# A two-layer graph network on one core: B, C and step sizes of the mixer's scan taken into wider products, a bias added by DMA, weights fetched through a ring

## The chip, the core and the metric

The kernel runs on one core of a Trainium2 chip, as one launch. The metric is the device time in microseconds of one execution, and a kernel's time is the median of several runs. The engines are TensorE (PE; its loads of the stationary operand are listed as PEld), VectorE (DVE), ScalarE (ACT), GpSimd (POOL) and SyncE (SP). Each works through a queue of its own in order, and DMAs are issued from the queues of SP and POOL. L637 is line 637 of the kernel before.

## The reference, cut to what matters

There are 32 graphs of 512 nodes with 256 features, and a 512 x 512 adjacency matrix for each. Two layers run one after the other; in each a graph part and a feed-forward part are added to x.

```python
# layer 0
x = x + graph_conv(layernorm(x), adj)                    # relu(x W_upd + mean of neighbours' x W_msg + bias)
t = max_over_features(xn[:, None, :] + Wt) + bt          # "tropical" product, 1024 outputs; xn = layernorm(x)
trop = s * max_k(t*sl_cvx + of_cvx) + (1-s) * min_k(t*sl_ccv + of_ccv)
g = sigmoid(xn @ Wg + bg)
x = x + (g*trop + (1-g)*gelu(xn @ Wc + bc)) @ Wd + bd
# layer 1
x = x + relu(softmax(leaky(masked e_src+e_dst)) @ h + bias) + h   # 4 heads, then a layer norm of each head
fx, xm = xn @ W_fx.T + b_fx, xn @ W_x.T + b_x            # 8 heads of 64
sw = softmax((xm @ W_slice.T + b_slice) / temp)          # each node's share of 64 slices
st = (fx, sw) summed over nodes / (sum of sw + 1e-5)     # 64 slice tokens of 512 features a graph
z, xBC, dt = split(st @ hy_in_w.T)                       # 512, 512+64+64, 2*8 columns, in this order
dt = softplus([dt[:8], flip(dt[8:])] + dt_bias)          # one step size a head and direction
x_, Bm, Cm = split(silu(causal_conv3(xBC)))
y = state-space scan of (dt, Bm, Cm, x_) over the 64 tokens, forward and backward, shifted by one
y = (y + x_ * (x_ @ fcD_w.T + D)) * silu(z)
y = y * rsqrt(mean(y*y) + 1e-5) * norm_w @ hy_out_w.T
x = x + (y handed back to the nodes by sw) @ out_w.T + out_b
```

## The kernel before

**Two layers, woven.** Everything is float32 except masks and adjacency. The program is written with Python generators: `woven` (L66) takes steps from two of them in a given proportion, and so sets the program order. A tile scheduler then places semaphores and may put an instruction of an engine ahead of others that are not ready. `tile_kernel` (L2165) runs `layer0_sorted` (L98), which weaves in the first part of `layer1_plain` (L865) as `following`, and then the rest of `layer1_plain`. Plainer versions of both layers (L705, L1614) stand under a condition at the end and are not entered with this input.

**Layer 0.** The graphs are taken in 4 segments of 8. `convs` makes the graph convolution of a segment, and its nodes are then sorted by how many terms their tropical maximum may need, and written to DRAM (`rows_of`). `feed_forwards` (L543) works on 32 groups of 4 tiles of 128 sorted nodes; a group is `xs`, 128 partitions by 4 rows. Its steps are `sums`, `mixed` and `down`, and the `sums` of the next group are woven with the `mixed` of the present one.

- `sums` (L546) gathers the group's nodes by POOL (L553), normalises them on ACT (xn, L574), and gathers for each node the row of a table that belongs to its largest feature (`best`, L564). For as many further terms as a tile needs (its cap less one) a row is gathered (`rows`, L595, four buffers) and taken into the maximum by DVE (L598). Last, POOL adds the bias bd of the final product to the four tiles one by one (L609 and L610). The normalised copy has been read by then, so that x + bd stands ready for the final sum.
- `mixed` (L613) computes for each 128 of the 1024 hidden features the two products (L623), their activations (L625), the transposed maximum (tz), the bends of the convex and concave functions (L632, L636 on ACT and L637 on DVE) and the gate's mixture.
- `down` (L645) multiplies by Wd (po, L652), DVE adds po to `xs`, and SP writes the group to `x2s`.

**Set-up of layer 1.** In `following` the constants of layer 1 come by SP's queue, each with a wait for its buffer. `load_T` (L999) takes a weight matrix in pieces of 128 rows: a DMA of up to 256 KB on SP's queue to one of two buffers (`raw512` and others), up to four PE transposes, and a copy by ACT. It is called for W_fx (4 pieces), hy_in_w (10, the last with 16 rows), hy_out_w (4), out_w (2) and fcD_w (1), with a yield after each piece. Then the small ones follow: W_slice, W_x and their biases, from which `wsl` is made (L1051). `add_rows` (L947) adds a constant row to a graph's x with one accumulating DMA from DRAM on POOL's queue (L949), whose source is a [2, 4 x 256] tile read by all partitions.

**Layer 1.** `attentions` goes through the graphs; `mixer` (L1580) through 16 groups g of two graphs. For each `want` that the mixer yields, credit times PACE steps of `attentions` are taken (end of `layer1_plain`), so that attention of later graphs fills the places where a mixer's step waits for another engine. The parts:

- `prepare` (L1155) gathers x, makes the attention's operands and, by PE, the mask (`maskp`, L1091).
- `attention` (L1223) goes in turns over pairs of heads q and blocks j of 128 neighbours. `weigh` (L1215) makes two weights `att` (L1220, DVE). After the last pair of a block, 12 matrix products are issued: eight into `avp` (L1256) and four into `adp` (L1261), in the order in which the weights were made. `norm` (L1289) follows some steps later.
- `slices` (L1325) makes the softmax over slices and `tokens` (L1365) the slice tokens uT.
- `scan` (L1390) is the mixer's recurrence, written as matrix products for both graphs of a group at once. Its order on PE is: xp, the x columns (L1407); bcp, B and C as two 64-column products (L1416); dtp, the step sizes (L1435, 32 records of 8 columns that put each head's direction in its place, and L1400); zp, the gate's 512 columns (L1400); then, after other work, gp = B C (L1494); segp, the summed logarithms (L1498); xtp and qp, which need the convolved x; yp (L1524); yTp; oTp (L1542); msp, the mean square spread over partitions (L1550); and vp. On DVE and ACT: softplus of the step sizes (Exp at L1450, Ln at L1456, and four DVE operations between); Silu of z (L1462); the four x convolutions of three taps (xT, each with a Silu); the convolutions of B and of C (bcT, cpad) on 64 partitions, each with a Silu; la and seg (L1488); decay (Exp of segp); mix and its three products; y and its products; the copies of yT and oT; and rms by POOL's power (after L1553).
- `unslice` (L1569) hands the result to the nodes (outp, L1574), and SP writes the graph out.

The few lines on which the prediction's steps rest are the bias loop, the step sizes and the attention's order:

```python
                for t in range(NT):
                    nc.gpsimd.tensor_add(xg[:, t, :D], xg[:, t, :D], bd)
...
            tok_matmul(pd[:, 2 * H : 4 * H], DT0, 2 * H)
            nc.vector.tensor_add(v, pd[:, : 4 * H], dtb.rearrange("p i h -> p (i h)"))
...
                    for p in range(AP):
                        for k in range(2 * HO // HW):
```

Of the kernel before, what the change touches and what calls it, by code (L numbers as in the profile page):

```python
# [8 lines left out]
F32 = mybir.dt.float32  # L9
# [4 lines left out]
AF = mybir.ActivationFunctionType  # L14
# [5 lines left out]
P = 128  # L20
# [77 lines left out]
def layer0_sorted(tc, ident, eps, x, adj, w, x2s, ranks, over, following):  # L98
# [29 lines left out]
    with ExitStack() as ctx:  # L128
# [12 lines left out]
        bd = const("bd", [P, D], w["bd"].partition_broadcast(P))  # L141
# [35 lines left out]

        table = dr.tile([D, FFN], F32, tag="table", name="table", bufs=1)
# [364 lines left out]
        def feed_forwards():  # L543


            def sums(s, g):  # L546
# [62 lines left out]
                for t in range(NT):  # L609
                    nc.gpsimd.tensor_add(xg[:, t, :D], xg[:, t, :D], bd)  # L610
# [254 lines left out]
def layer1_plain(tc, ident, eps, x2s, ranks, adj, w, out, over, ps):  # L865
# [35 lines left out]
    with ExitStack() as ctx:  # L901
# [58 lines left out]
        bc_w = const("bc_w", [S, 2, KW], w["hy_conv_w"][DI:].rearrange("(c p) k -> p c k", p=S))  # L960
        bc_b = const("bc_b", [S, 2], w["hy_conv_b"][DI:].rearrange("(c p) -> p c", p=S))
        skip = const("skip", [P, H], w["hy_D"].partition_broadcast(P))
        dtb = ctile("dtb", [P, 4, H])
        for i in range(4):
            nc.sync.dma_start(dtb[:, i, :], w["hy_dt_bias"].partition_broadcast(P))
# [31 lines left out]
        with tc.tile_pool(name="raw", bufs=2, side="right") as raw:  # L997

            def load_T(dst, src, name):  # L999

                R, Ccols = src.shape
                for r0 in range(0, R, P):
                    n = min(P, R - r0)
                    t = raw.tile([P, Ccols], F32, tag=f"raw{Ccols}", name=f"{name}_{r0}")
                    nc.sync.dma_start(t[:n], src[r0 : r0 + n, :])
                    pt = psum("tp", f"{name}p{r0}").rearrange("p (c r) -> p c r", r=P)
                    cs = Ccols // P
                    for c in range(cs):
                        nc.tensor.transpose(pt[:, c, :n], t[:n, c * P : (c + 1) * P], ident[:n, :n])
                    nc.scalar.copy(dst[:, :, r0 : r0 + n], pt[:, :cs, :n])  # L1010
                    yield

            yield from load_T(wfxT, w["W_fx"], "wfx")
            yield from load_T(inT, w["hy_in_w"], "in")
            yield from load_T(hoT, w["hy_out_w"], "ho")
            yield from load_T(owT, w["out_w"], "ow")
            yield from load_T(fcT, w["hy_fcD_w"], "fc")
# [5 lines left out]
            def twice_T(src, name):  # L1023

                R, Ccols = src.shape
                t = raw.tile([P, 2, Ccols], F32, tag="twice", name=name)
                for i in range(2):
                    nc.sync.dma_start(t[:R, i, :], src)
                pt = psum("tp", f"{name}p")
                nc.tensor.transpose(pt[:, :R], t[:R].rearrange("p i c -> p (i c)"), ident[:R, :R])  # L1030
                return pt


            wsT = raw.tile([P, G], F32, tag="wsT", name="wsT")
            nc.vector.tensor_copy(wsT, twice_T(w["W_slice"], "ws")[:, :G])
            wx = raw.tile([P, KC, D], F32, tag="wx", name="wx", bufs=1)
            nc.sync.dma_start(wx, w["W_x"].rearrange("(k p) d -> p k d", p=P))
            bx = raw.tile([P, KC], F32, tag="bx", name="bx")
            nc.sync.dma_start(bx, w["b_x"].rearrange("(k p) -> p k", p=P))
            bsl = raw.tile([1, H, G], F32, tag="bsl", name="bsl", bufs=1)  # L1040
            bs = raw.tile([1, G], F32, tag="bs", name="bs")
            nc.sync.dma_start(bs, w["b_slice"].rearrange("(o n) -> o n", o=1))
# [22 lines left out]
            for c in range(DC):  # L1065
                sq = raw.tile([P, H * G], F32, tag="wsl2", name=f"wsl2_{c}")
                nc.vector.tensor_mul(sq, wsl[:, c, :], wsl[:, c, :])
                nc.tensor.matmul(pn, ones, sq, start=c == 0, stop=c == DC - 1)
# [154 lines left out]
        def attention(b):  # L1223
# [21 lines left out]
            for i, (q, j) in enumerate(turns):  # L1245
# [5 lines left out]
                if q + 1 == AP:  # L1251
                    ends = dict(start=j == 0, stop=j == NT - 1)
                    for p in range(AP):
                        for k in range(2 * HO // HW):
# [5 lines left out]
                    for h in range(AH):  # L1260
# [129 lines left out]
        def scan(g, uT):  # L1390
# [14 lines left out]
            for k in range(KC):  # L1405
                for c in range(KC):
                    nc.tensor.matmul(px[:, k * T : (k + 1) * T], inT[:, c, DI + k * P : DI + (k + 1) * P],  # L1407
                                     uT[:, c, :], start=c == 0, stop=c == KC - 1)
# [3 lines left out]
            pb = psum("any", f"bcp{g}")  # L1412
            for i in range(2):
                c0 = 2 * DI + i * S
                for c in range(KC):
                    nc.tensor.matmul(pb[:S, i * T : (i + 1) * T], inT[:, c, c0 : c0 + S], uT[:, c, :],  # L1416
                                     start=c == 0, stop=c == KC - 1)
            bpad = sb.tile([S, 2, GB, LP], F32, tag="bpad", name=f"bpad{g}", bufs=1)
            nc.gpsimd.memset(bpad[:, :, :, : KW - 1], 0.0)
            nc.scalar.copy(bpad[:, :, :, KW - 1 :],  # L1420
                           pb[:S, : 2 * T].rearrange("p (k j l) -> p k j l", k=2, j=GB))
# [9 lines left out]
            pd = psum("any", f"dtp{g}")  # L1431
            for j in range(GB):
                for i in range(2):
                    for c in range(KC):
                        nc.tensor.matmul(pd[i * G : (i + 1) * G, j * H : (j + 1) * H],  # L1435
# [811 lines left out]
```

## Time and profile before

The page describes one profiled execution.

| what | value |
|---|---|
| median of 3 runs, us | 4365.9 (4364.42 to 4366.94) |
| profiled execution, us | 4372.35, its span 4370.6 |
| granted clock of PE, mean of the span | 0.955 |
| instructions in the span | 57973 |
| DMA packets | 244051, 507.52 MB, mean 116 GB/s |
| queue of POOL's software DMAs | 349.50 MB, 26.7% of the 16 engines' time |
| queue of SP's DMAs | 154.21 MB, 11.3% |
| rows gathered, L595 | 212 by 1166 ns of POOL |
| maximum, L598 | 212 by 1290 ns of DVE, idle before it 121.4 us |

The span is the time from the first to the last instruction. A row of instruction groups gives the line, the engine, the operation, the written tile and what it reads, how often it ran, its busy time, the mean duration of one in ns, and the idle time of its engine just before it with what ended most of this. The page's slices cut the span into 40 equal parts, and each digit is the busy share in tenths. In a timeline a row gives the start in us, the busy time, the engine, the line, the tiles, the shape and the number of instructions. A matrix product of the program shows as two records on PE; the tables count records.

### The profile page before, as it was taken

How to read it: one execution, taken by the hardware profiler on the slowest of the kernel's cores; microseconds unless marked ns; L12 is line 12 of the kernel's file. 1: busy time of each engine (PE TensorE's matmuls, PEld its weight loads, DVE VectorE, ACT ScalarE, POOL GpSimd, SP SyncE). 2: the span in 40 equal slices, each digit the busy share in tenths (PEclk: the TensorE clock that was granted, in tenths of full speed). 3: DMA queues.
4: the chain of work that ended last, by engine and by line, in shares of the span. 5: the costliest groups of instructions: out<-in, count | busy, mean ns of one | idle time of the engine just before them, and what ended most of it. 6: DMA issues, size and time to landing. Idle time of an engine off the chain costs nothing.

```text
span 4370.6 us, 57973 instructions
## 1 busy us (share of the span) xinstructions
PE 3882.4 (89%) x20311; PEld 2456.1 (56%) x20311; DVE 3279.3 (75%) x7008; ACT 2295.0 (53%) x4756; POOL 1617.9 (37%) x2036
## 2 busy tenths in 40 slices
PE   5567898988989999888998899999999999999997
PEld 4454565565655666554555455655555555555555
DVE  6668887898878978877775777777777777777763
ACT  3345655566655656546564555555554455554533
POOL 2346644665536644354431322222222222222210
PEclk8778999999999999998999999999999999999998
DMA  5546543564436644375441322222222322222200
GB/s 128 160 154 216 179 156 126 165 218 143 153 117 199 199 156 135 93 250 167 147 133 40 95 73 73 69 65 72 68 68 76 78 75 78 64 74 77 61 25 21
DMA packets 244051, 507.52 MB, mean 116 GB/s; under 512 B 39299, under 2 KB 114827, under 8 KB 243748
## 3 DMA queue, kind: packets, MB, share of 16 engines
q0 software_dynamic: 107904, 349.50, 26.7%
q1 hardware_dynamic: 135844, 154.21, 11.3%
q8 instruction: 162, 2.65, 0.2%
q14 instruction: 141, 1.16, 0.1%
HBM read 446.46 MB, written 57.17 MB: 115 GB/s over the span
## 4 chain that ended last, share of the span: by engine, by line
DVE 33%; PE 32%; DMA 11%; issue 9%; POOL 8%; ACT 5%; SPq 0%; another core or an unknown queue 0%; DVEq 0%; POOLq 0%; ACTq 0%
DVE att L1220 4%; DVE acc L637 4%; PE clsp L623 4%; PE gatep L623 3%; PE po L652 3%; PE avp L1256 3%; DMA rows<-table,xs 2%; DVE best L598 2%; DMA rows<-table,tops 2%; DVE sw L1349 2%; DVE sst L1347 2%; PE yTp L1354 2%; DVE sw L1344 2%; PE oTp L1542 1%; DMA best<-table,xs 1%
## 5 line engine op out<-in xcount | busy, mean ns | idle before, releaser
L623 PE MATMUL clsp<-xnT,wc 128*128 128x512 f32 x1024 | 521.8, 628 | 55.5 <-ACT cls L625 39.7
L623 PE MATMUL gatep<-xnT,wg 128*128 128x512 f32 x1024 | 502.1, 609 | 10.5 <-ACT gate L625 9.7
L652 PE MATMUL po<-wd,acc 128*128 128x256 f32 x2048 | 456.9, 382 | 6.5 <-DVE acc L641 3.5
L652 PEld LDWEIGHTS po<-wd,acc 128*128 128x128 f32 x2048 | 388.8, 191 | 73.1 <-issue 9.2
L1220 DVE SCALAR_TENSOR_TENSOR att<-own,other,mask 128x512 f32<-128x512 f32 x512 | 366.1, 744 | 76.4 <-DMA own<-ownd 76.4
L637 DVE SCALAR_TENSOR_TENSOR acc<-past,fld,acc 128x512 f32<-128x512 f32 x448 | 346.3, 776 | 28.3 <-ACT past L636 20.3
L598 DVE SCALAR_TENSOR_TENSOR best<-rows,xs,best 128x1024 f32<-128x1024 f32 x212 | 273.1, 1290 | 121.4 <-ACT best L592 75.8
L632 ACT ACTIVATE acc<-tz,fld 128x512 f32<-128x512 f32 x256 | 199.0, 778 | 269.1 <-PE tz L630 237.5
L623 PEld LDWEIGHTS gatep<-xnT,wg 128*128 128x128 f32 x1024 | 197.3, 197 | 254.0 <-issue 200.8
L636 ACT ACTIVATE past<-tz,fld 128x512 f32<-128x512 f32 x448 | 291.6, 694 | 73.6 <-DVE acc L637 72.1
L595 POOL DMA_INDIRECT rows<-table,xs x212 | 247.3, 1166 | 176.7 <-DVE best L598 121.8
L1256 PE MATMUL avp<-att,hv 128*32 128x512 f32 x2048 | 297.4, 599 | 6.1 <-DVE att L1220 6.1
L623 PEld LDWEIGHTS clsp<-xnT,wc 128*128 128x128 f32 x1024 | 182.6, 199 | 195.2 <-issue 114.3
L434 PE MATMUL pm<-h,adj 128*128 128x258 f32 (+1 forms) x1024 | 178.9, 321 | 100.3 <-DVE keep L427 34.4
L625 ACT ACTIVATE gate<-gatep,fld 128x512 f32<-128x512 f32 x256 | 175.6, 686 | 153.4 <-PE gatep L623 130.4
L1342 PE MATMUL lgp<-wsl,x4T 128*128 128x512 f32 x512 | 241.4, 610 | 14.3 <-ACT sw L1343 6.7
L1354 PE MATMUL yTp<-sw,x 128*128 128x512 f32 x512 | 237.0, 602 | 17.4 <-DVE sw L1349 16.9
L1161 POOL DMA_INDIRECT x<-x2s,ranks x128 | 135.2, 1056 | 295.5 <-DVE att L1220 147.5
L553 POOL DMA_INDIRECT xs<-rows_of,order x128 | 158.8, 1241 | 229.7 <-DVE acc L637 111.8
L1307 POOL TENSOR_TENSOR mu<-mu,eps 128x16 f32<-128x16 f32 x32 | 111.3, 3478 | 350.4 <-DVE mu L1306 350.4
L1574 PE MATMUL outp<-v,swT 128*128 128x256 f32 x1024 | 227.6, 381 | 0.0
L625 ACT ACTIVATE cls<-clsp,fld 128x512 f32<-128x512 f32 x256 | 176.3, 689 | 94.4 <-PE clsp L623 59.1
(598 smaller groups left out, 8809.0 us busy)
## 6 DMA issues: line engine op xcount, KB each, us to landing
adj<-in_adj POOLq DMA_DIRECT2D x128, 256.0 KB
ai<-in_adj SPq DMA_DIRECT2D x128, 256.0 KB
x<-added POOLq DMA_DIRECT2D x64, 512.0 KB
own<-ownd SPq DMA_DIRECT2D x128, 256.0 KB
rows_of<-keep SPq DMA_DIRECT2D x32, 550.0 KB
x<-in_x SPq DMA_DIRECT2D x32, 512.0 KB
x2s<-xs SPq DMA_DIRECT2D x32, 512.0 KB
out<-x SPq DMA_DIRECT2D x32, 512.0 KB
```

The source lines that it names most:

```text
L595: nc.gpsimd.indirect_dma_start(out=row, out_offset=None, in_=table, in_offset=bass.IndirectOffsetOnAxis(ap=idxs[:, k : k + 1].bitcast(U32) ...
L598: nc.vector.scalar_tensor_tensor(m, row, vals[:, k : k + 1], m, ALU.add, ALU.max)
L623: nc.tensor.matmul(pf, wf[:, c, f * P : (f + 1) * P], xnT[:, c, :], start=c == 0, stop=c == DC - 1)
L625: nc.scalar.activation(o, pf, fn, bias=fld[:, f, bf : bf + 1], scale=1.0 if fn == AF.Gelu else 0.5)
L636: nc.scalar.activation(r, z, AF.Relu, bias=fld[:, f, AT + b : AT + b + 1])
L637: nc.vector.scalar_tensor_tensor(y, r, fld[:, f, CH + b : CH + b + 1], y, ALU.mult, ALU.add)
L652: nc.tensor.matmul(po[:, i, :], acc[f][:, t * P : (t + 1) * P], wd[:, f, :], start=f == 0, stop=f == FC - 1)
L1220: nc.vector.scalar_tensor_tensor(e, own[h], other[:, j, h : h + 1], mask[:, j, :], ALU.max, ALU.mult)
L1256: nc.tensor.matmul(pv[p][k * HW : (k + 1) * HW, :], hv[:, j, h, e : e + HW], weighed[b, h, j], **ends)
L1342: nc.tensor.matmul(pf, xnT[:, c, t * P : (t + 1) * P], wsl[:, c, :], start=c == 0, stop=c == DC - 1)
L1354: nc.tensor.matmul(py, xn[:, t, c * P : (c + 1) * P], sw[:, t, :], start=t == 0, stop=t == NT - 1)
L1574: nc.tensor.matmul(po[:, :D], swT[:, k, t * P : (t + 1) * P], v[:, k, :], start=k == 0, stop=k == KC - 1)
```

## The change

It has four parts.

1. **Layer 0's last bias.** bd is put into a DRAM tile of four rows at the start. Instead of four POOL additions a group, one accumulating DMA a group is issued by POOL: its source is read by all partitions, and it writes four pieces of 256 elements on each partition, since a row of `xs` is longer than its 256 features.
2. **Layer 1's weights.** One list of 21 pieces replaces the calls of `load_T`. Their buffers are a ring of five, and the DMA of a piece is issued three pieces ahead of its use. In `inT` the columns of the step sizes come first, so that they lie next to the gate's. W_x, W_slice and their biases are asked for ahead of the pieces.
3. **Attention.** The 12 products of a block are issued in the reverse order of the weights: the weight made last is read first.
4. **The mixer's scan.** B and C are one product of 128 columns. The 16 step-size columns and the first 256 of the gate are one product of 272 columns into the same PSUM bank as B and C, and the other 256 are a product into a second bank. The 32 records of 8 columns go. DVE adds the bias to the 16 columns once and puts the four 64 x 8 blocks for the directions in place by four small additions. The convolution of B and C is one on 128 partitions instead of two on 64, and stands ahead of x's in the program; Silu of z is taken in two halves, and both stand ahead of all of these. gp's and yp's products alternate between the two graphs. The msp products go; four small DVE operations put the mean square in place instead.

The diff, cut to its core:

```diff
-        bd = const("bd", [P, D], w["bd"].partition_broadcast(P))
+        bd = dr.tile([NT, D], F32, tag="bd", name="bd", bufs=1)
+        nc.sync.dma_start(bd, w["bd"].partition_broadcast(NT))
...
-                for t in range(NT):
-                    nc.gpsimd.tensor_add(xg[:, t, :D], xg[:, t, :D], bd)
+                nc.gpsimd.dma_start(xg[:, :, :D], bd.partition_broadcast(P), accum_op=ALU.add)
...
+            wx = raw.tile([P, KC, D], F32, tag="wx", name="wx", bufs=1)
+            nc.sync.dma_start(wx, w["W_x"].rearrange("(k p) d -> p k d", p=P))
+            twice = raw.tile([P, 2, w["W_slice"].shape[1]], F32, tag="twice", name="ws", bufs=1)
...
-            yield from load_T(wfxT, w["W_fx"], "wfx")
-            yield from load_T(inT, w["hy_in_w"], "in")
-            yield from load_T(hoT, w["hy_out_w"], "ho")
-            yield from load_T(owT, w["out_w"], "ow")
-            yield from load_T(fcT, w["hy_fcD_w"], "fc")
+            pieces = [(dst, src, r0)
+                      for dst, src in ((wfxT, w["W_fx"]), (inT[:, :, 2 * H :], w["hy_in_w"][:DT0]),
+                                       (inT[:, :, : 2 * H], w["hy_in_w"][DT0:]), (hoT, w["hy_out_w"]),
+                                       (owT, w["out_w"]), (fcT, w["hy_fcD_w"]))
+                      for r0 in range(0, src.shape[0], P)]
+            def fetch(i):
...
+                t = raw.tile([P, DI], F32, tag="piece", name=f"piece{i}", bufs=5)
+                nc.sync.dma_start(t[:n, : src.shape[1]], src[r0 : r0 + n, :])
+                return t
+            coming = [fetch(i) for i in range(3)]
+            yield
+            for i, (dst, src, r0) in enumerate(pieces):
+                if i + 3 < len(pieces):
+                    coming.append(fetch(i + 3))
...
+                    nc.tensor.transpose(pt[:, c, :n], coming[i][:n, c * P : (c + 1) * P], ident[:n, :n])
+                nc.scalar.copy(dst[:, :, r0 : r0 + n], pt[:, :cs, :n])
+                yield
...
-                    for p in range(AP):
-                        for k in range(2 * HO // HW):
+                    for p in reversed(range(AP)):
+                        for k in reversed(range(2 * HO // HW)):
...
-                    for h in range(AH):
+                    for h in reversed(range(AH)):
...
-            pb = psum("any", f"bcp{g}")
-            for i in range(2):
-                c0 = 2 * DI + i * S
-                for c in range(KC):
-                    nc.tensor.matmul(pb[:S, i * T : (i + 1) * T], inT[:, c, c0 : c0 + S], uT[:, c, :],
-                                     start=c == 0, stop=c == KC - 1)
+            pb, pz = psum("any", f"bcp{g}"), psum("any", f"zp{g}")
+            for c in range(KC):
+                nc.tensor.matmul(pb[:, :T], inT[:, c, DIN - P :], uT[:, c, :], start=c == 0, stop=c == KC - 1)
+            first = 2 * H + DI // 2
+            tok_matmul(pb[:, T : T + first], 0, first)
+            tok_matmul(pz[:, : DI // 2], first, DI // 2)
...
-            pd = psum("any", f"dtp{g}")
-            for j in range(GB):
-                for i in range(2):
-                    for c in range(KC):
-                        nc.tensor.matmul(pd[i * G : (i + 1) * G, j * H : (j + 1) * H],
-                                         uT[:, c, j * G : (j + 1) * G],
-                                         inT[:, c, DT0 + i * H : DT0 + (i + 1) * H],
-                                         start=c == 0, stop=c == KC - 1)
-            tok_matmul(pd[:, 2 * H : 4 * H], DT0, 2 * H)
+            pd = pb[:, T : T + 2 * H]
...
-            nc.vector.tensor_add(v, pd[:, : 4 * H], dtb.rearrange("p i h -> p (i h)"))
+            nc.vector.tensor_add(v[:, 2 * H :], pd, dtb.rearrange("p i h -> p (i h)"))
+            for i in range(2):
+                for j in range(GB):
+                    half = slice(j * G, (j + 1) * G)
+                    nc.vector.tensor_add(v[i * G : (i + 1) * G, j * H : (j + 1) * H],
+                                         pd[half, i * H : (i + 1) * H], dtb[half, 0, :])
...
-            pz = psum("any", f"zp{g}")
-            tok_matmul(pz, 0, DI)
-            nc.scalar.activation(z, pz, AF.Silu)
+            nc.scalar.activation(z[:, : DI // 2], pb[:, T + 2 * H : T + first], AF.Silu)
+            nc.scalar.activation(z[:, DI // 2 :], pz[:, : DI // 2], AF.Silu)
+            conv(bpad, bc_w, bcT)
+            for half, dst in ((slice(0, S), bcT[:S]), (slice(S, P), cpad[:, :, 1 : G + 1])):
+                nc.scalar.activation(dst, bcT[half], AF.Silu, bias=bc_b[half])
...
-            for i in range(2):
-                conv(bpad[:, i], bc_w[:, i, :], bcT[:, i])
-                dst = bcT[:, 0] if i == 0 else cpad[:, :, 1 : G + 1]
-                nc.scalar.activation(dst, bcT[:, i], AF.Silu, bias=bc_b[:, i : i + 1])
...
-            for j in range(GB):
-                half = slice(j * G, (j + 1) * G)
-                for h in range(H):
+            for h in range(H):
+                for j in range(GB):
+                    half = slice(j * G, (j + 1) * G)
                     nc.tensor.matmul(py[half, h * C : (h + 1) * C], heads(mix)[half, h, :],
                                      heads(xk)[half, h, :], start=True, stop=True)
...
-            pm = psum("any", f"msp{g}")
+            rms = sb.tile([P, GB], F32, tag="rms", name=f"rms{g}")
             for j in range(GB):
                 for i in range(P // C):
-                    nc.tensor.matmul(pm[i * G : (i + 1) * G, j : j + 1], ident[:, j * G : (j + 1) * G], ms,
-                                     start=True, stop=True)
-            rms = sb.tile([P, GB], F32, tag="rms", name=f"rms{g}")
-            nc.vector.tensor_scalar(rms, pm[:, :GB], 1.0 / DI, LN_EPS, ALU.mult, ALU.add)
+                    nc.vector.tensor_scalar(rms[i * G : (i + 1) * G, j : j + 1], ms[j * G : (j + 1) * G], 1.0 / DI, LN_EPS,
+                                            ALU.mult, ALU.add)
```

## What the change should do to the time: the prediction

> **What bounds it now.** I read the page's shares, its slices, the chain of waits, and then the timelines of PE, ACT and DVE around one mixer scan.
>
> ```profile
> PE 3882.4 (89%) x20311; PEld 2456.1 (56%) x20311; DVE 3279.3 (75%) x7008; ACT 2295.0 (53%) x4756; POOL 1617.9 (37%) x2036
> PE   5567898988989999888998899999999999999997
> DVE  6668887898878978877775777777777777777763
> DVE 33%; PE 32%; DMA 11%; issue 9%; POOL 8%; ACT 5%; SPq 0%; another core or an unknown queue 0%; DVEq 0%; POOLq 0%; ACTq 0%
> ```
>
> One slice is 109 us. From slice 24 on (layer 1, about 2500 us on) PE stands at 9 throughout: each of the mixer's 16 groups takes some 118.5 us (start of xp to the next), and the gaps in PE's timeline are 4 to 5 us of it. There PE instructions are worth their own time, unless a wait replaces them. In slices 4 to 22 (layer 0) PE, DVE and POOL take turns on the chain.
>
> The scan of group 8, the pattern of most groups:
>
> ```profile
> 3490.80 1.02 PE L1256 MATMUL avp<-att,hv 128*32 128x512 f32 x2
> 3491.76 3.84 PE L1407 MATMUL xp<-uT,inT 128*128 128x128 f32 x32
> 3495.52 1.96 PE L1416 MATMUL bcp<-uT,inT 128*64 128x128 f32 x16
> 3497.32 1.36 PE L1435 MATMUL dtp<-inT,uT 128*64 128x8 f32 x32
> 3498.61 1.07 PE L1400 MATMUL dtp<-inT,uT 128*128 128x16 f32 x8
> 3499.53 3.68 PE L1400 MATMUL zp<-inT,uT 128*128 128x512 f32 x8
> 3503.04 0.83 PE L1091 MATMUL maskp<-identb,a 128*128 128x128 bf16 x12
> ...
> 3509.09 0.46 PE L1494 MATMUL gp<-cpad,bcT 64*64 64x64 f32 x8
> 3509.48 1.42 PE L1498 MATMUL segp<-seg,seg_l 128*64 128x512 f32 x4
> ...
> 3517.96 1.90 PE L1524 MATMUL yp<-xk,mix 64*64 64x64 f32 x32
> ...
> 3523.16 3.84 PE L1542 MATMUL oTp<-yT,hoT 128*128 128x128 f32 x32 [0.89 <-ACT yT L1536]
> 3526.93 0.40 PE L1550 MATMUL msp<-ms,ident 128*64 128x1 f32 x8
> ```
>
> Matmuls overlap, so I price by the distance of starts, not by the printed length. One written matmul is two records.
>
> **Mixer, PE's side.** From bcp's start to zp's end PE issues for 3503.04 - 3495.52 = 7.52 us. After: 8 records of 128x128 at xp's 3.76/32 = 0.1175 us (0.94), 8 of 272 columns at about hp's (264 columns, 2.68/12 = 0.223) 0.23 (1.84), 8 of 256 at outp's 7.01/32 = 0.219 (1.75): 4.53. **Saved 2.99 us.** In yp the two 64x64 tiles alternate instead of 16 records each in a row; now 1.83/32 = 0.057 apart; rnp, which alternates, stands 0.036 apart: 1.15, saved 0.67 (bounds 0 and 0.9). gp likewise, 0.1. msp's 0.33 us buys nothing: oTp to vp is 4.51 us in this scan and vp needs ACT's copy of oTp (3.84 + 0.08 + 0.59 + 0.04 = 4.55), so msp lies inside a wait. Attention reversed: the first matmul waits for the fourth weight instead of the first, with all 24 records queued behind it. In layer 1's steady part the trace has no idle PE for att, and in all 6.1 us; I take 0, bounds -5 and +8. But the two extra matmuls move: in the program order of the changed kernel four matmuls (8 records, 0.87 us) stand ahead of xp where one (2 records) stood, in a hole of about 0.7 us in which PE waited for uT. So 6 records, 0.65 us, leave the later stretch for nothing, and xp starts some 0.15 late.
>
> If PE alone decided, a scan would give 2.99 + 0.67 + 0.65 = 4.3 us.
>
> **Mixer, what is late next.** The queues of ACT and DVE do not allow it.
>
> ```profile
> 3504.15 1.28 ACT L1450 ACT_TABLE_LOAD   x1
> 3505.44 0.23 ACT L1450 ACTIVATE sp<-sp 128x32 f32<-128x32 f32 x1
> 3505.69 1.28 ACT L1462 ACT_TABLE_LOAD   x1
> ...
> 3508.50 1.27 DVE L1488 TENSOR_TENSOR seg<-la,seg_r 128x512 f32<-128x512 f32 x2
> 3511.34 1.01 POOL L31 TENSOR_TENSOR rsd<-rsd,eps 128x4 f32<-128x4 f32 x1
> ```
>
> Before, seg ends at 3509.7, when PE comes to segp (3509.48): no slack. I walk the new order with these durations, in us from xp's start. PE: zp done 8.3, then 8 masks, 32 attention matmuls (64 records at 0.113, 7.2), at gp by 16.4 to 17 (a mask also waits for the bank of bcp, which z's first half holds to 10.4). ACT: four xT with their load to 9.4, one a, both halves of z to 10.4, Exp with load 11.9, ai 12.5, Silu load and bcT 14.1, Ln with load 15.6, Silu load and cpad **17.3**. DVE: av ends 6.0 (it waits for POOL's mu, as before), twelve conv 8.9, x 10.0, five sp adds 0.43 (one before; four 64x8 pieces at 0.08), three bcT instead of six, three masks, two att, norm statistics to 16.8; then shiftd stands **ahead of seg** in the new order and waits for POOL's pow (1.4 us from last mvd to shiftd before): 18.2; seg 18.3 to 19.5. So gp starts about 17.4 and segp 19.0 (17.7 before). From there xtp, qp, DVE's dq and five 128x512 products (3.2 us) reach yp at 25.3 (26.2 before), yp takes 0.67 less, oTp starts at 29.9 plus the 0.15 instead of 31.4: **1.4 us a scan** out of 4.3. Eight groups (1, 2, 4, 5, 7, 8, 10, 11) have this order. In 6, 9, 12 and 13 shiftd is earlier (17.5), seg 18.4, but ACT's three x outputs and another mask precede decay and mix: yp 25.5 against 25.1 before, less 0.67: 0.2 each. Groups 0, 3, 14: about 1 each. Group 15 has no other work: ACT's loads bring cpad at 17.2 against 17.3, gain yp alone, 1.5. Sum 8 x 1.4 + 4 x 0.2 + 3 + 1.5 = **16.5 us**. The four rms pieces on DVE cost 0.3 us beside oTp.
>
> A rule is against this order: the Trainium skill ("ScalarE: Activation LUTs", What ACT_TABLE_LOAD costs) has a switch at 1283 ns plus a drain of about 1380. The count is six a scan before and after, but now four lie in series before cpad. By the rule cpad comes 4 x 1.38 = 5.5 us later, at 22.8, and all scans lose about 4 us (65 us slower). The trace shows the activation 1.29 us after the load began and the next load 0.02 us after an activation's end: I take the row.
>
> **L0's bias.** 128 POOL adds go, 32 accumulating DMAs come, also on POOL's queue.
>
> ```profile
> L610 POOL TENSOR_TENSOR xs<-xs,bd 128x256 f32<-128x256 f32 x128 | 109.3, 859 | 165.9 <-ACT xn L574 164.8
> L637 DVE SCALAR_TENSOR_TENSOR acc<-past,fld,acc 128x512 f32<-128x512 f32 x448 | 346.3, 776 | 28.3 <-ACT past L636 20.3
> ```
>
> Two gains. Pairing starts and ends in the timelines: the 50 L637 that overlap an L610 take 1034 ns, the others 745 in the median; over all DVE rows that excess is 45 us. On the chain of waits lie 21.5 us of that excess and 13.6 us of L610 itself: **35 us**. One wait for the last xn stays where there were four. Cost: the nearest row is L949, the same kind of DMA with the same 512 KB: 0.93 us of POOL each, 30 us in all, an eighth on the chain as L610 was (4 us). Its 4 KB packets take about 0.34 us against a gather's 0.16, and it lands 4.6 to 6.5 us after issue; the skill's fit ("DMA: Bandwidth & Descriptors", Anatomy of one DMA - SWDGE), 2.0 + bytes/436e3, would say 3.2. By the row the 16 engines are held 8 x 0.34 = 2.7 us, by the rule 1.2: gathers issued behind it (L595, L553) come that much later, 32 times. Four row buffers hide part; DMA has 15% of layer 0's chain, but right behind the add a gather is often next, so I take a third: 32 x 2.7/3 = 29 us at worst and 11 as my value (half of these in groups with one or two rows, which wait for nothing). Here the rows are four pieces of 1 KB, which no row shows: POOL's issue may cost from 0.93 to 4 x 0.93 us. I take 0.93. Net 35 - 4 - 11 = **20 us** (bounds -45 and +25).
>
> **L1's weights.** PE waits for their DMAs 4.1 (wfx), 7.4 (in) and 3.2 (ho): 14.7 us. The ring fetches three ahead; five buffers cover the first five, but fourteen pieces now stand almost in a row on PE (0.87 us each), while each 256 KB came 2.9 us apart before, beside gathers. Most of the wait comes back: gain **4 us** (bounds 13 gain, 8 loss). wx and W_slice move ahead of the pieces on SP's queue and delay the first by some 2 us, inside that bound.
>
> **Sum.** 16.5 + 20 + 4 = 40.5 us. The profiled execution is 4372.35 us (span 4370.6 and 1.75 around it), 6.4 over the median of 4365.9: 4331.9 by its own time, 4325 by the median.
>
> **Rivals.**
> 1. PE gets its 4.3 us: 16 x 4.3 + 24 = 93 us, **4273**. For it: PE is at 9 in every slice of layer 1. Against: gp and segp had no slack, and seg stands behind a POOL round trip. Chance 0.22, with all between.
> 2. The accumulating DMA is dear, the slower side: POOL's queue takes 3.7 us for 512 pieces (32 x 2.8 = 89 us more, half of it on the chain where gathers queue behind), and gathers lose the full 29 us: layer 0 loses 45 + 29 + 4 - 35 = 43 us, the mixer gives 20: **4389**. It decides from about 1.7 us a DMA lost on the chain beyond my value (40/32 = 1.3 makes it even). For it: the bias row is cut in 1 KB pieces. Chance 0.10.
> 3. The chain refills: layer 0's chain changes hands so often that a removed DVE or POOL piece lets another wait end last, and only the mixer's part stays, less the ring's loss: 8 to 12 us, **4356**. Chance 0.08.
>
> My forecast has 0.60. Its own range is 4300 to 4345; with the rivals **4276 to 4362**. A difference under 0.2%, 8.7 us, can't be told from none. Faster: 0.58 + 0.22 + 0.04 = 0.84; same: 0.02 of the forecast, 0.02 of rival 2, 0.04 of rival 3 = 0.08; slower 0.08.
>
> **What would show it.** xp to zp's last start 8 us instead of 11; idle PE before gp and segp of 2 us or more where it was 0; xp to oTp near 30 us (27 means rival 1); POOL's busy time 70 to 85 us less (none: rival 2); L637 near 745 ns; L595's rows waited for by DVE more than the present 83 us; PE's waits for the pieces 5 to 12 us. Wrong if layer 0's end (last po) does not come 10 us earlier, or a scan's idle PE stays at 1 us.

## The result, and the profile after

The changed kernel takes 4338.8 us (median of 6 runs, 4335.2 to 4344.6) where the one before takes 4365.2 us in the same comparison: a ratio of 0.9944, 95% interval 0.9928 to 0.9960, so 24 us less (17 to 31). The forecast was 40.5 us less; its range of 4276 to 4362 holds the time. Its profiled execution has a span of 4342.9 us. The page's shares, two of its slices and its chain:

```profile
PE 3828.5 (88%) x19543; PEld 2428.8 (56%) x19543; DVE 3241.5 (75%) x7072; ACT 2294.3 (53%) x4771; POOL 1546.6 (36%) x1940
PE   5568998899989999888997899999999999999987
DVE  6668887797778977886775777867777777777763
DVE 24%; PE 14%; POOL 7%; issue 5%; ACT 4%; DMA 4%; POOLq 0%; DVEq 0%; ACTq 0%; SPq 0%
```

PE has 53.9 us less to do. The chain's shares add up to 58% where they were 98%, so this chain was lost on the way and is not set against the earlier one. The starts of PE's own products divide the two profiled executions better (us; the groups are those of the mixer, from xp to xp):

| stage | before | after | difference |
|---|---|---|---|
| layer 0, to the end of the last po | 2387.9 | 2347.1 | -40.8 |
| start of layer 1, to xp of group 0 | 149.2 | 156.5 | +7.3 |
| groups 0 to 13 | 1663.6 | 1668.5 | +4.9 |
| groups 14, 15 and the end | 169.9 | 170.8 | +0.9 |

So layer 0 gained more than the 24 us that I gave to the bias and the ring, and the mixer, to which I gave 16.5 us, gave nothing. (Layer 0 alone can differ by some 15 us between executions: a kernel in which nothing of it was changed ended it 15.2 us earlier than this profile of before. The stages therefore say where to look, and the timed comparisons below say how much.)

The scan of group 8 again, now in the timeline of the changed kernel:

```profile
3457.49 3.84 PE L1412 MATMUL xp<-uT,inT 128*128 128x128 f32 x32
3461.17 1.06 PE L1419 MATMUL bcp<-uT,inT 128*128 128x128 f32 x8
3462.06 2.00 PE L1404 MATMUL bcp<-inT,uT 128*128 128x272 f32 x8
3463.90 1.89 PE L1404 MATMUL zp<-inT,uT 128*128 128x256 f32 x8
...
3467.71 0.68 DVE L1442 TENSOR_TENSOR sp<-bcp,dtb 64x8 f32<-64x8 f32 x4
3468.43 0.38 ACT L1456 ACTIVATE z<-bcp 128x256 f32<-128x256 f32 x1 [0.51 <-DVE sp L1442]
3468.83 1.28 ACT L1445 ACT_TABLE_LOAD   x1
...
3475.53 0.40 ACT L1463 ACTIVATE cpad<-bcT,bc_b 64x128 f32<-64x128 f32 x1
3475.98 0.45 PE L1493 MATMUL gp<-cpad,bcT 64*64 64x64 f32 x8 [1.04 <-ACT cpad L1463]
...
3477.08 2.48 PE L1497 MATMUL segp<-seg,seg_l 128*64 128x512 f32 x4 [0.65 <-DVE seg L1487]
3484.96 1.15 PE L1523 MATMUL yp<-xk,mix 64*64 64x64 f32 x32 [0.27 <-DVE mix L1516]
3489.41 3.84 PE L1541 MATMUL oTp<-yT,hoT 128*128 128x128 f32 x32 [0.89 <-ACT yT L1535]
```

The three products end some 8 us after xp's start instead of 11, and yp takes 1.15 us instead of 1.90. Then PE stands 1.04 us before gp, which waits for cpad, and 0.65 us before segp, which waits for seg; before, gp waited for nothing. And segp takes 2.48 us where it took 1.42, with the same four records of the same shape. Nothing in the program explains that. The granted clock does.

### The profile page after: what moved, and what is told of

Same layout as the page of the kernel before. It is cut to its first block, busy times and chain, and to the rows that moved or that the text cites. A ratio compares the mean times of both kernels' runs of the same rounds, so it can differ in the third digit from the quotient of the medians.

```text
span 4342.9 us, 56442 instructions
## 1 busy us (share of the span) xinstructions
PE 3828.5 (88%) x19543; PEld 2428.8 (56%) x19543; DVE 3241.5 (75%) x7072; ACT 2294.3 (53%) x4771; POOL 1546.6 (36%) x1940
## 3 DMA queue, kind: packets, MB, share of 16 engines
q14 instruction: 140, 1.15, 0.1%
## 4 chain that ended last, share of the span: by engine, by line
DVE 24%; PE 14%; POOL 7%; issue 5%; ACT 4%; DMA 4%; POOLq 0%; DVEq 0%; ACTq 0%; SPq 0%
DVE att L1223 5%; DVE sw L1353 2%; PE clsp L623 2%; DVE sst L1351 2%; DVE sw L1348 2%; PE gatep L623 2%; PE yTp L1358 2%; PE oTp L1541 2%; POOL x L1164 1%; DVE mask L1095 1%; POOL mu L1311 1%; DMA x<-x2s,ranks 1%; PE outp L1571 1%; PE po L652 1%; PE vp L1561 1%
## 5 line engine op out<-in xcount | busy, mean ns | idle before, releaser
L637 DVE SCALAR_TENSOR_TENSOR acc<-past,fld,acc 128x512 f32<-128x512 f32 x448 | 331.6, 744 | 37.9 <-ACT past L636 29.9
L1260 PE MATMUL avp<-att,hv 128*32 128x512 f32 x2048 | 274.0, 603 | 21.9 <-DVE att L1223 21.9
```

What stands on the lines that cost most here:

```text
L637: nc.vector.scalar_tensor_tensor(y, r, fld[:, f, CH + b : CH + b + 1], y, ALU.mult, ALU.add)
L1260: nc.tensor.matmul(pv[p][k * HW : (k + 1) * HW, :], hv[:, j, h, e : e + HW], weighed[b, h, j], **ends)
```

## The hole and the clock

Group 5 has the same instructions and the same two waits, ahead of gp and of segp, in two profiled executions of the changed kernel. Windows of the first (the first row is the whole period, the others are 2 us long; the columns are: length, then busy time and instructions of PE, PEld, DVE, ACT, POOL, then PEclk, the granted clock, and DMA):

```profile
3098.50:3218.00 119.50, 112.60 (x723) 68.61 (x719) 87.70 (x203) 61.71 (x159) 30.05 (x28) 0.97 0.27 71
3115.00:3117.00 2.00, 0.96 (x14) 0.05 (x2) 1.00 (x8) 1.87 (x3) 1.11 (x2) 1.00 0.00 0
3117.00:3119.00 2.00, 1.35 (x11) 0.64 (x12) 1.57 (x4) 1.65 (x4) 0.20 (x2) 0.96 0.00 0
3119.00:3121.00 2.00, 2.00 (x7) 0.79 (x5) 0.00 (x0) 1.82 (x2) 0.00 (x0) 0.50 0.03 8
3121.00:3123.00 2.00, 2.00 (x12) 2.00 (x11) 0.13 (x2) 0.59 (x1) 0.00 (x0) 0.50 0.00 0
```

and of the second (the run named a2 below):

```profile
3098.60:3215.70 117.10, 110.75 (x722) 67.23 (x718) 87.80 (x203) 61.69 (x159) 30.06 (x28) 0.99 0.27 73
3117.00:3119.00 2.00, 1.22 (x11) 0.69 (x12) 1.57 (x4) 1.56 (x4) 0.38 (x2) 1.00 0.00 0
3119.00:3121.00 2.00, 2.00 (x15) 1.26 (x13) 0.00 (x0) 1.97 (x4) 0.00 (x0) 1.00 0.04 8
```

In the first, PE is less than half busy for some 3 us, then gets half its clock and does 7 records in 2 us; in the second it does 15. The period is 2.4 us longer in the first, which has 6.8 us at half clock in this group; the second has 3.4 us of it, later, from 3164.80 on. The same holds for other groups: in 2, 5, 8 and 11, oTp starts 31.9 to 33.3 us after xp in the execution that has half clock behind the hole, and 30.5 us after it in the other.

Over groups 0 to 13 PE's busy time, its idle time and the clock records of the traces add up to this (us):

| groups 0 to 13 | period | PE busy | PE idle | at half clock |
|---|---|---|---|---|
| before | 1663.6 | 1593.1 | 70.6 | 3.4 |
| after, first execution | 1668.5 | 1555.6 | 112.9 | 51.2 |
| after, second execution | 1660.9 | 1550.5 | 110.4 | 41.0 |

The two executions after differ by 10.2 us at half clock and by 5.1 us of busy time, so that half of such a stretch is added to PE's work. Taken off, 1530.0 us of work are left in both: 61 us less than before on the same count, where 14 scans at the forecast 4.3 us make 60. Of this saving the waits took 42 and 40 us, near the 46 us that the walk of the queues had left to them, and the half clock took 24 and 19 us more than before. The walk had promised a gain of some 14 us for these groups. It had the waits about right and did not have the clock at all, and that is where its gain went.

## The experiments

Ratios are to the kernel before, with a 95% interval; the medians of before were 4363.7, 4367.2 and 4367.1 us in the three comparisons.

**Each part alone.** The edits are the hunks of the diff shown above, one part at a time on the kernel before. The ring alone keeps the old order of columns in `inT`, and in the mixer alone `load_T` writes the new order:

```diff
-            yield from load_T(inT, w["hy_in_w"], "in")
+            yield from load_T(inT[:, :, 2 * H :], w["hy_in_w"][:DT0], "in")
+            yield from load_T(inT[:, :, : 2 * H], w["hy_in_w"][DT0:], "dt")
```

> Only the first part: layer 0's last bias by one accumulating DMA a group; everything else as before. Theory A (layer 0's gain of 41 us up to the last po is the removed additions and the DVE operations that they slowed): 25 to 35 us faster, the last po 25 us or more earlier, layer 1 unchanged. Theory B (the terms of the prediction were right, 20 us from the bias): 15 to 22 us faster. Theory C (the gain of layer 0 comes from the ring): under 10 us.

> Only the second part: layer 1's weights through a ring of five, columns of the step sizes where they were. Theory A: 5 to 12 us faster, all of it between 1850 and 2000 us, since PE's waits for these DMAs fall from 14.7 us to about 4. Theory B: 4 us. Theory C: 20 us or more.

> Only the third part: the products of a block read the weight made last first. Theory A (the first product now waits for the last weight where DVE is the late engine): 5 to 10 us slower, and PE's idle time before avp on DVE's att grows from 6.1 us to some 15 to 22 us in the first graphs of layer 1. Theory B: no difference, within 3 us.

> Only the fourth part: the mixer's scan, with the columns of the step sizes first in inT. Theory A (PE's saving of about 4 us a scan is spent in a wait for cpad of over 1 us before gp and of 1 us after it, and this hole pulls the granted clock to 0.5 for 3 to 10 us in about half of the groups): within 6 us of before, either sign; 4 to 8 of the 16 groups show a granted clock below 0.985. Theory B (the prediction's walk): 16 us faster, clock 0.99 to 1.00 in groups 0 to 13.

| part | ratio | us |
|---|---|---|
| bias by DMA | 0.9941 (0.9918 to 0.9964) | -26 (-36 to -16) |
| ring | 0.9974 (0.9965 to 0.9983) | -11 (-15 to -7) |
| attention | 0.9996 (0.9984 to 1.0008) | -2 (-7 to +3) |
| mixer | 1.0018 (1.0009 to 1.0027) | +8 (+4 to +12) |

Theory A holds for the bias. For the ring it holds for the time, but PE's waits for the pieces fell to 9.9 us and not to 4. It misses for attention, which was to be 5 to 10 us slower: its loss in the first graphs is there (PE's idle time before avp grew from 6.1 to 13.9 us, and 149.2 us became 151.7 up to xp of group 0), but groups 0 to 13 took 8.5 us less, in a profiled execution of 4350.2 us where the median of the 14 timed is 4361.2, and the sum can't be told from nothing.

For the mixer the wait is that of theory A, and the 8 us lie just outside its 6, though their interval reaches inside. Of low groups there are only two below 0.985 among groups 0 to 13 of this one profile (groups 5 and 9), not 4 to 8, and 20.5 us at half clock. But the profiled execution, 4358.8 us, has the shortest time and the highest granted clock of the 22 that were timed. Over these the clock of the whole execution runs from 0.946 to 0.954, and the time goes with it (correlation -0.76): the six at 0.948 or less have a median of 4376 us, the five at 0.951 or more one of 4367 us. At the median clock of 0.9495 some 40 us more are spent at half clock than in the profile (an estimate: 2 x 0.0045 x 4370 us).

**Is there a way to have PE's saving?** If cpad and seg are late because DVE and ACT begin with x, then the product that starts the long chain should come first. One move in the changed kernel:

```diff
+            pb = psum("any", f"bcp{g}")
+            for c in range(KC):
+                nc.tensor.matmul(pb[:, :T], inT[:, c, DIN - P :], uT[:, c, :], start=c == 0, stop=c == KC - 1)
+            first = 2 * H + DI // 2
+            tok_matmul(pb[:, T : T + first], 0, first)
...
+            nc.scalar.copy(bpad[:, :, KW - 1 :], pb[:, :T].rearrange("p (j l) -> p j l", j=GB))
             px = psum("any", f"xp{g}")
...
-            pb, pz = psum("any", f"bcp{g}"), psum("any", f"zp{g}")
-            for c in range(KC):
-                nc.tensor.matmul(pb[:, :T], inT[:, c, DIN - P :], uT[:, c, :], start=c == 0, stop=c == KC - 1)
-            first = 2 * H + DI // 2
-            tok_matmul(pb[:, T : T + first], 0, first)
+            pz = psum("any", f"zp{g}")
             tok_matmul(pz[:, : DI // 2], first, DI // 2)
...
-            nc.scalar.copy(bpad[:, :, KW - 1 :], pb[:, :T].rearrange("p (j l) -> p j l", j=GB))
```

> The changed kernel with one move: the product of B and C and that of the step sizes and half the gate are issued ahead of x's product, and bpad is copied before xpad. Theory A (the mixer lost because cpad and seg came late, and because the hole before them pulled the clock): gp starts at 16 us or less after the scan's first product or without a wait, idle PE before gp and segp under 0.5 us, no group from 1 to 13 with a granted clock below 0.985, and 10 to 25 us faster than the changed kernel, so 4315 to 4330. Theory B (the mixer's part costs by itself, through its DVE pieces or banks): within 5 us of the changed kernel's 4339.

4288.9 us, ratio 0.9820 (0.9803 to 0.9837): 78 us less than before, and 50 us less than the changed kernel, twice what I expected at most. The timeline of its group 8, where x's product starts at 3431.58:

```profile
3431.12 0.62 PE L1404 MATMUL bcp<-inT,uT 128*128 128x272 f32 x2
3432.22 0.69 DVE L1443 TENSOR_TENSOR sp<-bcp,dtb 64x8 f32<-64x8 f32 x4
...
3440.91 0.40 ACT L1464 ACTIVATE cpad<-bcT,bc_b 64x128 f32<-64x128 f32 x1
...
3442.08 0.45 PE L1494 MATMUL gp<-cpad,bcT 64*64 64x64 f32 x8
3443.06 1.58 PE L1498 MATMUL segp<-seg,seg_l 128*64 128x512 f32 x4 [0.54 <-DVE seg L1488]
```

DVE has put the step sizes in place while PE is still at x, cpad is ready 9.7 us after xp's first product instead of 18.4, gp waits for nothing, and segp, which waits 0.54 us and not under 0.5, takes 1.58 us. In the trace of groups 0 to 13, 10.2 us are left at half clock. Groups 0 to 13 take 1616.7 us instead of 1663.6: 3.4 us a group, of the 4.3 us that PE saves. Set against the first execution of the changed kernel (1668.5 us), PE's busy time is 25 us less, of which the clock explains 20, and its idle time 27 us less. So clock and wait have about equal parts in what the move gives back.

To see that this belongs to the mixer and not to its meeting with the other parts, the same move was made in the mixer alone:

> The fourth part alone, as in the run of the mixer alone that was 8 us slower than before, with the product of B, C and step sizes moved ahead of x's. Theory A (PE's saving of some 4 us a scan is real, and only the wait for cpad and seg with the clock took it): 40 to 55 us faster than before, 4310 to 4325. Theory B (the gain of the moved product came from its meeting with the other parts): under 25 us.

4311.8 us, ratio 0.9869 (0.9853 to 0.9885): 55 us faster than before where the mixer alone, with x first, was 8 us slower. Theory A, at the upper end. So PE's saving is real, and the order of two products, with the copy of bpad that goes with the first, decides whether it is had.

**Does the low clock move about?**

> The changed kernel once more, unaltered, beside the next one on the same chip. Theory A (its low clock in the mixer depends on how the hole before segp falls into the clock's own windows, so it varies from execution to execution): the groups with a granted clock below 0.985 are others than 1, 2, 3, 5, 6 and 13, or another number of them, and the time is 4330 to 4350. Theory B (something fixed in those groups lowers it): the same six groups.

4339.6 us, ratio 0.9942 (0.9923 to 0.9962). The low groups are now 1, 3, 6, 9 and 12: groups 2, 5 and 13 recovered (117.8 instead of 119.7 us, 117.1 instead of 119.5, 119.1 instead of 121.3), group 9 got it (121.4 instead of 119.6). Theory A.

**Filling the hole with work that nobody needs.** First before gp, then between gp and segp:

```diff
+            for i in range(4):
+                nc.tensor.matmul(pg[:G, 2 * G :], bcT[:S, 0, :], inT[:S, 0, : N - 2 * G], start=True, stop=True)
             for i in range(2):
                 for j in range(GB):
                     nc.tensor.matmul(pg[j * G : (j + 1) * G, i * G : (i + 1) * G], bcT[:S, j, :],
```
```diff
+            for i in range(3):
+                nc.tensor.matmul(pg[:G, 2 * G :], cpad[:, 0, :G], inT[:S, 0, : N - 2 * G], start=True, stop=True)
             pl = psum("any", f"segp{g}")
```

> The changed kernel with four products of 384 columns (8 records) more in each scan ahead of gp, whose result nobody reads: PE has about 1.3 us more to do a scan, 21 us in all, placed where it waits for cpad. Theory A (the low clock comes from the hole): the number of groups 1 to 13 with a granted clock below 0.985 falls from 6 to 2 or fewer, and the time is within 8 us of the changed kernel's 4339 or below it. Theory B (the clock has another cause): the low groups stay, and the time rises by 10 us or more.

> The changed kernel with three products of 384 columns (6 records) more between gp and segp in each scan, where PE waits for seg; nobody reads their result, and PE's order is otherwise that of the changed kernel. About 1 us of PE work a scan is added, of which the wait for seg takes 0.7 us. Theory A (the hole pulls the clock): groups 1 to 13 with a granted clock below 0.985 fall to 2 or fewer, and the kernel with more work is 8 to 25 us faster than the changed one. Theory B (the waits alone cost the time): 3 to 12 us slower than the changed one.

Both failed. The first takes 4370.1 us (0.9998, 0.9985 to 1.0011), the second 4365.9 (0.9999, 0.9989 to 1.0010): 31 and 26 us slower than the changed kernel. I had mispriced the filler: the eight records take 2.79 us instead of 1.3, the six 2.10 us instead of 1, so that the waits no longer covered them. In the first run 16 records of attention, which stood ahead of gp in the usual pattern, moved behind qp, and yp starts 27.2 us after xp instead of 26.0; in the second segp starts at 20.8 us instead of 19.6. The clock was not cured either: 34.1 and 37.5 us at half clock in groups 0 to 13. The number of low groups fell to two and three, as theory A had it for the first run, while the time rose as theory B had it. So these two runs do not show by an intervention that the clock alone is worth the time. The evidence for it is the pairs of equal groups, the busy times above, and the spread of the timed executions of the mixer alone.

**The smaller questions.** The order of yp's and gp's products alone, gp's likewise with i outside:

```diff
-            for j in range(GB):
-                half = slice(j * G, (j + 1) * G)
-                for h in range(H):
+            for h in range(H):
+                for j in range(GB):
+                    half = slice(j * G, (j + 1) * G)
```

> The kernel before with only the order of the yp and gp products changed, so that they alternate between the two graphs. Theory A (yp lies on PE's path in every scan): 0.7 us a scan, 8 to 12 us faster, yp's 32 records 0.036 us apart. Theory B (the saved time turns into a wait): under 3 us.

4362.5 us, ratio 0.9986 (0.9977 to 0.9994): 6 us faster, between the two theories; of the 0.75 us a scan that yp loses, about half arrives.

The first two parts together, with attention and scan as before:

> The first two parts together, attention and the scan as before. Theory A (the parts of layer 0 add up: 26 and 11 us): 4325 to 4330, faster than the changed kernel. Theory B (the two gains share waits): 4333 to 4340, no better than the first part alone.

4337.8 us, ratio 0.9934 (0.9918 to 0.9950): 29 us faster, the time of theory B, where 26 and 11 add up to 37. The intervals overlap, and whether the two share a wait stays open. It is as fast as the whole change, which is another way to say that the rest of the change brings nothing in its order.

Attention as before, in the kernel with B and C first (the three `reversed` taken out):

> The kernel with the product of B, C and step sizes first (4289 us), with the attention's products in the order of before. Theory A (reading the last weight first costs 5 to 8 us in the first graphs of layer 1 and gives it back later, about 0.8 us a group): within 5 us of 4289. Theory B (it is a loss): 6 to 10 us faster. Theory C (it is a gain): 6 us or more slower.

4280.3 us, ratio 0.9806 (0.9786 to 0.9827): 87 us faster than before, the fastest of all. The 8.5 us by which it beats the reversed order lie in the range of theory B, but the two intervals overlap, so that I can't say that the reversal costs anything; only that it brings nothing. In its profile no group from 0 to 13 has any time at half clock.

## Why the prediction was right, and where it was not

That the number came out within the range is in part luck, because two errors had opposite signs: the bias and the ring brought more than I gave them (13 us, each timed alone; 5 us, timed together), the mixer alone 24 us less.

- **PE's side of the mixer: right.** Zp's last record starts 7.9 us after xp's start (8 was forecast), yp takes 1.15 us (1.15). That msp lies in a wait is borne out too: PE's idle time from oTp to the end of outp grew from 0.14 to 0.56 us a scan.
- **What is late next: right in kind, 0.5 to 1.1 us short.** Forecast for most groups were gp at 17.4, segp at 19.0, yp at 25.3 and oTp at 30.0; groups that kept their clock (4, 7, 10) have 18.5, 19.6, 26.0 and 30.5, and before it was 31.4. So 0.9 us a scan, not 1.4. The term that was off is the one for the step sizes: four small additions at 0.08 us each. They take 0.16 to 0.17 us (the profile before already had 0.16 us for L1553, with two elements a partition, and 0.12 to 0.19 us for all but one of the operations on 128x32 in this chain), and by the trace's releaser ACT's Silu of the gate's first half, which reads the same bank, waits 0.51 us for them; both lie ahead of Exp in the chain to cpad. Groups 9 and 12, for which I forecast 0.2 us, lose: oTp at 32.0 against 31.05.
- **The step that failed is the mixer's sum of 16.5 us.** It priced the hole as a wait and stopped there. The sentence "idle PE before gp and segp of 2 us or more" was in the forecast, and came nearly true (1.24 and 0.63 us on average of groups 0 to 13, 1.9 us together); what it does to the products behind it was not. The runs put 41 to 51 us of half clock in groups 0 to 13 beside it, which added 19 to 24 us to PE's work.
- **The rule on table loads.** The walk by the trace's rows had cpad at 17.3, the rule's drain of 1380 ns at 22.8; it came at 18.4. The rows were the better guide: in the timeline above the load at 3468.83 is followed by its activation at 3470.12, 1.29 us later, as before.
- **Bias: 26 us instead of 20.** L637 fell to the 745 ns forecast. (The 1034 ns that the prediction set beside it is the mean of its 50 rows; their median is 936 ns.) The gain of 35 us was not measured apart from the costs, which were off on both sides.

```profile
L637 DVE SCALAR_TENSOR_TENSOR acc<-past,fld,acc 128x512 f32<-128x512 f32 x448 | 331.6, 744 | 37.9 <-ACT past L636 29.9
L610 POOL DMA_DIRECT2D xs<-bd x32 | 44.7, 1397 | 79.6 <-ACT xn L575 56.1 <-issue 13.4 <-ACT cls L625 9.8
```

  The issue takes 1.40 us of POOL and not the 0.93 us that I took, far from 4 times that; but the 11 us that I set aside for gathers behind it do not show: DVE waited 43.3 and 38.4 us for rows, and before 43.6 and 39.5. With 5.6 us for POOL (an eighth of 32 x 1.40) and nothing for the gathers, 35 us become 29, an estimate that the interval of 16 to 36 us holds.
- **Ring: 11 us instead of 4,** inside its bound of 13. The ring alone leaves PE 9.9 us of waits for these DMAs where it had 14.7, which explains 5 us; the rest of its gain was not traced.
- **Attention: 0, right** within the interval of 7 us less to 3 us more. The loss of 2.5 us before group 0 was not in the forecast; whether a gain behind it makes up for it is not shown.
- **The rivals.** The first, in which PE gets its 4.3 us a scan, was not this kernel but is the one with two products exchanged: its price of 4273 us stands beside 4289 and 4280 measured. The slower rival's two prices, a POOL issue of 3.7 us and delayed gathers, were both wrong. The third, a chain that refills in layer 0, is refuted by the bias alone.

## What to carry to other kernels

When products are taken off a PE that is the bound, find out what PE then waits for and make the product that feeds the longest chain of other engines the first, not the one whose consumer is largest: here the exchange of two products was worth 50 us, twice what the whole change gained. A wait on PE is not priced by its length alone; look at the granted clock in the microseconds behind it. And where work that differs by some 15 us between executions lies ahead of the part that was changed, as layer 0 does here, time each part alone before believing in a sum.

## What the hardware showed that was not expected

All stretches at half clock lie on one grid. These are the starts and lengths in us of those in groups 0 to 13, from the clock records of the trace:

```
changed kernel, first execution: 2640.98 6.83, 2760.45 3.41, 2808.23 3.41, 2879.91 6.83, 3118.84 6.83,
                                 3238.31 10.24, 3477.24 3.41, 3832.23 3.41, 4071.16 6.83
second execution:                2642.56 10.24, 2881.49 6.83, 3164.80 3.41, 3236.47 6.83, 3591.46 6.83, 3946.45 6.83
```

Within an execution the starts are whole multiples of 3.413 us apart (2760.45 - 2640.98 is 35.00 of them, 3477.24 - 2640.98 is 245.0), and the lengths are one, two or three of them; the two executions' grids lie differently to the program. I cut the traces of the kernel before, of both executions after and of the mixer alone into windows of that grid, some 1950 in all, and took the share of each in which PE had a record. Of the 20 windows at full clock that were followed by half clock the busiest had 0.508; of the others all but seven had 0.517 or more. So a grid window in which PE has records for about half of the time or less was followed by half clock in 20 of 27 cases, a fuller one never; why seven were spared is not known. In three traces that had no part in this count (B and C first, the same with attention as before, and in the mixer alone; 1421 windows) it was seven of nine, and again no fuller one.

This is why the groups change. The two waits, 1.04 and 0.65 us with gp between them, span 2.14 us, and PE has records for 44% of the 3 us about them. A window of 3.41 us that holds both waits is half empty, and 37% of its positions do ((3.41 - 2.14)/3.41, an estimate); half clock followed the hole in 13 of the 28 groups of the two executions. The emptiest 3.41 us from xp to 40 us behind it in group 8 have records for 0.74 of their time before, 0.50 after, and 0.64 with B and C first. The Trainium skill ("TensorE: Matmul & The Clock Gate", What's actually happening) describes this window, free-running and 3413 ns long, and the trace agrees to 0.01 us. Its advice to avoid idle gaps above some 3 us (Why this matters for your kernels) is too mild for this case: in group 5 no gap ahead of the half clock was longer than 1.04 us. In the two kernels with filler the share does not mark the windows: some with records in 0.55 to 0.74 of their time were followed by half clock as well; the filler used 64 rows and 64 columns of the array, but whether the share of the array counts was not tried.
